# A swin-attention and Fourier-mixing kernel: the attention's transposes for the next row move to the head of the full-array block, and the projection moves ahead of the next image's transposes

## The chip, the cores and the metric

The kernel runs on one core of one Trainium2 chip. The metric is the device time of one execution in microseconds (us), as the median of several runs. The five engines of the core are called by the profile's names: PE is the matrix engine (TensorE) and PEld its weight loads, DVE is VectorE, ACT is ScalarE, POOL is GpSimd, and SP is the engine whose queue issues most DMA transfers.

## The reference

The input is 32 images of 56 x 56 tokens with 128 channels, in float32. Two residual layers follow each other:

```
x = x + attention(group_norm(x))     # layer 0
x = x + fourier(group_norm(x))       # layer 1

attention: roll by (-3,-3); cut into 8 x 8 windows of 7 x 7 = 49 tokens
    qkv = win @ w_qkv.T                       # 4 heads of 32 channels
    a = softmax(q k^T * 32**-0.5 + bias + mask)
    out = (a @ v) @ w_proj.T + b_proj; windows back, roll by (3,3)

fourier: DCT along W, 32 modes, each mode mixed by w0, inverse DCT
    + the same along H with w1
    then relu(h @ W1 + b1) @ W2 + b2          # hidden size 512
```

Everything in an image depends on the norm over that whole image, so the kernel works on three images at a time: one is loaded and transposed, one goes through the attention row by row, one (or two) through the Fourier layer.

## The kernel before

Work goes in cycles. In one cycle, one row of 8 windows of the current image enters the attention (`attn_qk`, `attn_v`, `attn_scores`), the row of two cycles before leaves it (`attn_values`, `attn_project`), and the Fourier layer of the earlier images advances by one step. Eight cycles make one image. Below, "cycle i" is a cycle in which row i (0 to 7) enters.

The order of instructions on PE, ACT, DVE and POOL is the order in which the program writes them. A cycle is written in blocks by the way in which the PE array is divided: `full_first` (whole array), then half columns, quarters and eighths, then `full_last` (whole array again), which runs on into the next cycle's `full_first`. Half columns may come before or after quarters.

```python
def attn_bank():                       # PSUM of the attention: 4 banks in turn
    return bank("pa", 4)

def attn_exp(r):                       # ACT
    nc.scalar.activation(a3, a3, AF.Exp)

def attn_divide(r):                    # DVE sum and reciprocal, then POOL  (L443, L445, L446)
    nc.vector.tensor_reduce(sm, a3, axis=AX.X, op=ALU.add)
    nc.vector.reciprocal(rs, sm)
    nc.gpsimd.tensor_tensor(a3, a3, rs..., ALU.mult)

def attn_transpose(im, i, r):          # softmax rows to columns
    a = a_sb[r % 3]
    im.aT = []
    for hf in range(2):
        pt = attn_bank()
        for h in range(NH):
            nc.tensor.transpose(pt..., a..., ident...)         # L457, 8 in all
        aT = work.tile([P, 4, P], F32, tag="aT", name="aT")
        if hf: nc.scalar.copy(aT..., src)                      # L465, ACT
        else:  nc.vector.tensor_copy(aT..., src)               # L467, DVE
        im.aT.append(aT)

def attn_values(im, i, r):             # 32 small matmuls L482 into two banks, then
    ...                                # oT <- banks: ACT L515, three DVE L513

def attn_project(im, i):               # 3 or 4 matmuls L524 on oT, then
    ...                                # DVE L532 (xl += projection), DMA to scr

def image_groups(im, i):               # next image: 7 transposes L262 into two banks,
    ...                                # ACT copies xw (L280, L274, L275),
                                       # DVE statistics L284, POOL adds b_proj (L289)
```

```python
def full_first(cycle, norm):
    im, i = row(cycle - 2)
    if im:
        attn_transpose(im, i, cycle - 2)
    ...                                        # sums of the row of cycle - 3
    attn_qk(im, i, False)                      # row(cycle): PE L359 (q), L366 (k);
                                               # ACT L362 (q), L371 (k), DVE L379 (k)
    ...
    ff_in(im, FF_AT.index(c))                  # PE L749 (4 matmuls), ACT L757 (hid)
    ...
    attn_divide(cycle - 1)

def quarters(cycle):                           # PE L413, DVE L421; L706
    ...
def half_columns(cycle):                       # PE L391, ACT L398; L633 or L667
    ...
def eighths(cycle):                            # PE L482
    im, i = row(cycle - 2)
    if im:
        attn_values(im, i, cycle - 2)

def full_last(cycle, norm):
    next(norm)
    if row(cycle - 2)[0]:
        last_out(cycle)                        # ff_out: PE L769, DVE L781
    next_image(cycle)                          # image_groups in cycles 3, 4, 5 and 6
    if row(cycle)[0]:
        attn_exp(cycle)                        # ACT L438
    im, j = row(cycle - 2)
    if im:
        attn_project(im, j)
    next(norm)
```

The row maximum and its subtraction (`attn_max`: DVE L431, POOL L432) stand after the eighths in cycles without a feed-forward group and before the half columns in cycles with one. The feed-forward runs in seven of the eight cycles, with groups of 512 tokens and, in cycles 6 and 7, of 320 and 256; cycle 5 has none.

```python
FF_GROUPS = (HB, HB, HB, HB, 320, 256, HB)     # HB = 512
FF_AT = (7, 8, 9, 10, 12, 13, 14)              # step of the Fourier layer; step = cycle number - 10 - 8 * image
```

Of the kernel before, what the change touches and what calls it, by code (L numbers as in the profile page):

```python
# [23 lines left out]
WT = WS * WS  # L24
# [11 lines left out]
JP = 64  # L36
# [12 lines left out]
def swin_fourier_kernel(  # L49
# [33 lines left out]
    def attn_bank():  # L83
        return bank("pa", 4)
# [24 lines left out]
    def load_image(b):  # L109
        t = big.tile([TC, NCH, C], F32, tag="xl", name="xl", bufs=2)  # L110
        h = NCH // 2
        for n0, n1 in ((0, h), (h, NCH)):
            for a, e, p, src in chunks_of(x, b, n0, n1):
                nc.sync.dma_start(t[p, a:e], src)
        return t
# [128 lines left out]
    def image_begin(b):  # L244
        im = Image()
        im.b = b
        im.x = xls.pop(b) if b in xls else load_image(b)
        im.xw = {}
        im.st = small.tile([P, NWR, 6], F32, tag="st0", name="st0", bufs=2)
        im.part = small.tile([TC, 2, C // 4, NWR], F32, tag="part", name="part", bufs=1)  # L250
        im.scr = dram.tile([S, S, C], F32, tag="scr", name="scr", bufs=2)
        return im
# [197 lines left out]
    def attn_transpose(im, i, r):  # L450

        a = a_sb[r % 3]
        im.aT = []
        for hf in range(2):
            pt = attn_bank()
            for h in range(NH):
                nc.tensor.transpose(  # L457
                    pt[:PW, h * P : h * P + PW],
                    a[:PW, h, 2 * hf : 2 * hf + 2].rearrange("p w j -> p (w j)")[:, :PW],
                    ident[:PW, :PW],  # L460
                )
            aT = work.tile([P, 4, P], F32, tag="aT", name="aT")
            src = pt[:PW].rearrange("p (m x) -> p m x", x=P)[:, :, :PW]
            if hf:
                nc.scalar.copy(aT[:PW, :, :PW], src)  # L465
            else:
                nc.vector.tensor_copy(aT[:PW, :, :PW], src)  # L467
            im.aT.append(aT)

    def attn_values(im, i, r):  # L470


        v = v_sb[r % 3]
        po = [attn_bank(), attn_bank()]
        HALF = RT // 2
        po4 = [p[:, :HALF].rearrange("p (r n s) -> p n r s", r=WS, s=WS) for p in po]
        for f in range(2):
            for e in range(2):
                for h in range(NH):
                    for u in range(2):  # L480
                        ks = slice(u * JP, u * JP + WT)
                        nc.tensor.matmul(  # L482
                            po4[u][h * HD : (h + 1) * HD, 2 * f + e],
                            lhsT=v[ks, 2 * f + e, h * HD : (h + 1) * HD],
                            rhs=im.aT[f][ks, h, e * JP : e * JP + WT],
                            start=True,
                            stop=True,
                        )

        if i % 2 == 0:  # L490
            im.oT = work.tile([P, 2 * RT], F32, tag="oT", name="oT")
        oT = im.oT


        oTr = oT[:, i % 2 * RT : (i % 2 + 1) * RT].rearrange("p (r x) -> p r x", x=S)
        for u in range(2):
            src = po[u][:, :HALF].rearrange("p (r f x) -> p r f x", r=WS, f=2)
            x0 = SS + u * 2 * WS
            if not u:
                dst = bass.AP(  # L500
                    oTr.tensor, oTr[:, :, x0:].offset, [oTr.ap[0], [S, WS], [4 * WS, 2], [1, 2 * WS]]
                )
                parts = [(dst, src)]
            else:
                n = S - 4 * WS - x0
                parts = [
                    (oTr[:, :, x0 : x0 + 2 * WS], src[:, :, 0]),
                    (oTr[:, :, S - n : S], src[:, :, 1, :n]),
                    (oTr[:, :, 0:SS], src[:, :, 1, n:]),
                ]  # L510
            for d, f in parts:
                if u:
                    nc.vector.tensor_scalar(d, f, im.bias[:, 2:3], None, ALU.add)  # L513
                else:
                    nc.scalar.activation(d, f, AF.Identity, bias=im.bias[:, 2:3])  # L515

    def attn_project(im, i):

        oT = im.oT
        n0, n1 = WS * i // 2, WS * (i + 1) // 2  # L520
        base = i // 2 * WS
        pp = attn_bank()
        for n in range(n0, n1):
            nc.tensor.matmul(  # L524
                pp[:TC, (n - n0) * C : (n - n0 + 1) * C],
                lhsT=oT[:, (n - base) * TC : (n - base + 1) * TC],
                rhs=wproj,
                start=True,
                stop=True,
            )  # L530
        piece = im.x[:, n0:n1]
        nc.vector.tensor_tensor(  # L532
            piece,
            pp[:TC, : (n1 - n0) * C].rearrange("p (n c) -> p n c", c=C),
            piece,
            ALU.add,
        )
        nc.sync.dma_start(
            im.scr[2 * n0 : 2 * n1].rearrange("(n r) w c -> (r w) n c", r=2), piece
        )  # L540
# [273 lines left out]
    def row(r):  # L814
        return (images[r // NWR], r % NWR) if 0 <= r < NB * NWR else (None, 0)

    def fourier(cycle):

        b, c = divmod(cycle - CONV_BEGIN, NWR)
        return [(images[b - k], c + k * NWR) for k in (1, 0) if 0 <= b - k < NB]  # L820
# [5 lines left out]
        return []  # L826

    def full_first(cycle, norm):
        im, i = row(cycle - 2)
        if im:  # L830
            attn_transpose(im, i, cycle - 2)
        last, j = row(cycle - 3)
        if last:
            sums = attn_sums(last, j)
            next(sums)
        im, i = row(cycle)
        if im:
            attn_qk(im, i, False)
        for im, c in fourier(cycle):
            for width, g in back_groups(c):  # L840
                load_modes(im, width, g)
        next(norm)
        if last:
            next(sums)
        for im, c in fourier(cycle):
            if c == 0:
                im.stats = fourier_stats(im)
                im.cols = {}
                next(im.stats)
                load_columns(im, 0)  # L850
                load_columns(im, 1)
        for im, c in fourier(cycle):
            if c in FF_AT:
                ff_in(im, FF_AT.index(c))
        for im, c in fourier(cycle):
            if c == 0:
                next(im.stats)
        if row(cycle - 1)[0]:
            attn_divide(cycle - 1)
# [29 lines left out]
    def eighths(cycle):  # L889
        im, i = row(cycle - 2)  # L890
        if im:
            attn_values(im, i, cycle - 2)

    def last_out(cycle):
        for im, c in fourier(cycle):
            if c in FF_AT:
                ff_out(im, FF_AT.index(c))

    def full_last(cycle, norm):
        next(norm)  # L900
        if row(cycle - 2)[0]:
            last_out(cycle)
        next_image(cycle)
        if row(cycle)[0]:
            attn_exp(cycle)
        im, j = row(cycle - 2)
        if im:
            attn_project(im, j)
        next(norm)

    def next_image(cycle):
        b, i = divmod(cycle, NWR)
        if b + 1 < NB:
            if i == 2:
                images[b + 1] = image_begin(b + 1)
            for j in {3: (0,), 4: (2,), 5: (4,), 6: (6,)}.get(i, ()):
                image_groups(images[b + 1], j)
# [3 lines left out]
    def first_rows(cycle, norm):  # L921
        im, i = row(cycle)
        if im:
            attn_qk(im, i, True)
        if cycle:
            attn_exp(cycle - 1)
        next(norm)
        last, j = row(cycle - 3)
        if last:
            attn_project(last, j)  # L930
        im2, i2 = row(cycle - 2)
        if im2:
            attn_transpose(im2, i2, cycle - 2)
        if cycle:
            attn_divide(cycle - 1)
        if im:
            attn_scores(im, i, cycle)
            attn_max(cycle)
        if im2:
            attn_values(im2, i2, cycle - 2)  # L940
        if last:
            for _ in attn_sums(last, j):
                pass
        if im:
            attn_v(im, i, cycle)
        next(norm)
        next_image(cycle)
        if cycle == CONV_BEGIN - 1:
            attn_exp(cycle)
            attn_project(im2, i2)  # L950
        next(norm)

    def nothing():
# [4 lines left out]
    with tc.manual_schedule(engines={ET.PE, ET.Activation, ET.DVE, ET.Pool}):  # L958
# [6 lines left out]
        for cycle in range(NB * NWR + CONV_BEGIN + FF_AT[-1] - NWR + 1):  # L965
# [21 lines left out]
            b, i = divmod(cycle, NWR)  # L987
# [66 lines left out]
```

## Time and profile before

| What | Value |
|---|---|
| median of 3 runs | 3668.28 us (3667.28 to 3670.64) |
| span of the profiled run | 3669.3 us |
| instructions | 139900 |
| DVE busy | 2222.3 us (61%) |
| ACT busy | 2152.8 us (59%) |
| POOL busy | 1371.9 us (37%) |
| mean granted PE clock | 0.996 |
| HBM traffic over the span | 103 GB/s |

Busy times are sums over the whole span. Where one engine waits for another, the row of waits names the waiting instruction, the one that released it, and the total, the number and the longest of these waits. A timeline row has the start, the duration, the engine, the source line, what is written from what, the shapes, how often it is repeated without a break, and in brackets the idle time before it with the instruction that ended it. A matmul on float32 data can appear as two records. Durations of successive PE rows overlap, because a matmul's end is modelled and the next one starts before it; so the time that a group takes on PE is read here as the difference between the starts of two rows that follow each other.

### The profile page before, as it was taken

The page shows a single profiled execution, that of the slowest core. Times are in us where ns is not written, and L with a number is a line of the kernel's source. Part 1 is how long each engine was busy: PE and PEld are TensorE (multiplying, and loading weights), DVE is VectorE, ACT ScalarE, POOL GpSimd, SP SyncE. Part 2 cuts the span into 40 slices and gives each one's busy share as a digit, 9 for nine tenths or more (in the row PEclk, how much of TensorE's full clock was granted, in tenths as well). Part 3 has the DMA queues.
Part 4 walks back from the last instruction along what each step waited for, and adds up shares of the span by engine and source line. Part 5 has one row for each costly group of instructions (what it writes and reads, how often), then busy time and mean ns, then how long its engine had stood idle before and what let it go on. Part 6 is the DMA issues. An engine that isn't in the chain of part 4 may idle for free.

```text
span 3669.3 us, 139900 instructions
## 1 busy us (share of the span) xinstructions
PE 3603.8 (98%) x61184; PEld 2938.0 (80%) x61184; DVE 2222.3 (61%) x4741; ACT 2152.8 (59%) x4043; POOL 1371.9 (37%) x1421
## 2 busy tenths in 40 slices
PE   7899999999999999999999999999999999999998
PEld 5687888888888888888888888878888888888786
DVE  7766666656666566666566665666656666656641
ACT  5565556655565656566555666565665565665653
POOL 5433334333334333343333343333343333433321
PEclk9999999999999999999999999999999999999999
DMA  4334443433433334334434334443344343443333
GB/s 116 97 102 111 107 109 93 118 106 102 115 97 106 108 106 113 105 98 118 106 101 117 97 108 107 109 111 99 103 110 110 102 115 98 111 108 106 96 108 90
DMA packets 687795, 388.93 MB, mean 106 GB/s; under 512 B 40495, under 2 KB 658128, under 8 KB 686928
## 3 DMA queue, kind: packets, MB, share of 16 engines
q1 hardware_dynamic: 686573, 379.65, 38.1%
q8 instruction: 482, 7.90, 0.9%
q14 instruction: 129, 1.06, 0.1%
q10 hardware_dynamic: 611, 0.32, 0.0%
HBM read 218.29 MB, written 161.48 MB: 103 GB/s over the span
## 4 chain that ended last, share of the span: by engine, by line
PE 91%; DVE 4%; ACT 2%; POOL 1%; issue 1%; DMA 0%; SPq 0%; POOLq 0%; DVEq 0%; ACTq 0%
PE pc L769 21%; PE pc L749 17%; PE pa L391 7%; PE pc L667 6%; PE pc L633 6%; PE pa L413 6%; PE pa L457 5%; PE pc L706 5%; PE pa L524 5%; PE pa L482 4%; PE pa L359 4%; PE pa L366 4%; PE pa L262 2%; POOL a L432 1%; DVE a L421 1%; DVE mx L431 1%
## 5 line engine op out<-in xcount | busy, mean ns | idle before, releaser
L769 PE MATMUL pc<-wff,hid 128*128 128x128 f32 (+1 forms) x6400 | 779.1, 279 | 1.0 <-ACT hid L757 0.9
L446 POOL TENSOR_TENSOR a<-a,rs 128x784 f32<-128x784 f32 x256 | 389.6, 1522 | 993.0 <-DVE rs L445 869.7
L769 PEld LDWEIGHTS pc<-wff,hid 128*128 128x128 f32 (+1 forms) x6400 | 731.1, 189 | 24.0 <-issue 2.9
L749 PE MATMUL pc<-xf,wff 128*128 128x512 f32 (+2 forms) x1792 | 710.9, 539 | 0.9 <-DVE xf L717 0.6
L757 ACT ACTIVATE hid<-pc,b1sb 128x512 f32<-128x512 f32 (+2 forms) x896 | 536.4, 635 | 93.0 <-PE pc L749 89.4
L749 PEld LDWEIGHTS pc<-xf,wff 128*128 128x128 f32 x1792 | 339.5, 190 | 310.3 <-issue 229.4
L432 POOL TENSOR_TENSOR a<-a,mx 128x784 f32<-128x784 f32 x256 | 388.8, 1519 | 456.9 <-DVE mx L431 448.0
L781 DVE TENSOR_TENSOR res<-pc,res 128x512 f32<-128x512 f32 (+3 forms) x259 | 144.1, 568 | 607.7 <-issue 293.9
L289 POOL TENSOR_TENSOR xl<-xl,bproj 112x512 f32<-112x512 f32 (+1 forms) x256 | 286.0, 1138 | 347.3 <-PE pa L262 338.8
L421 DVE TENSOR_TENSOR a<-pa,bm 128x392 f32<-128x392 f32 x512 | 259.7, 550 | 203.2 <-PE pa L413 203.1
L438 ACT ACTIVATE a<-a 128x784 f32<-128x784 f32 x256 | 225.0, 879 | 222.3 <-POOL a L432 221.9
L379 DVE TENSOR_SCALAR k<-pa,heads,bqkv 128x392 f32<-128x392 f32 x246 | 168.6, 685 | 288.0 <-ACT k L371 288.0
L465 ACT COPY aT<-pa 113x452 f32<-113x452 f32 x256 | 137.5, 537 | 303.0 <-PE pa L457 298.7
L398 ACT COPY v<-pa 128x512 f32<-128x512 f32 x256 | 152.5, 596 | 268.4 <-PE pa L391 268.3
L739 POOL TENSOR_TENSOR res<-res,b2sb 128x512 f32<-128x512 f32 (+2 forms) x256 | 263.7, 1035 | 98.5 <-DMA res<-scr 88.3
L413 PEld LDWEIGHTS pa<-k,q 64*64 64x64 f32 x8192 | 183.6, 132 | 137.7 <-DVE rs L445 67.5
L513 DVE TENSOR_SCALAR oT<-pa,bqkv 128x98 f32<-128x98 f32 (+2 forms) x768 | 170.6, 278 | 200.0 <-PE pa L482 200.0
L391 PE MATMUL pa<-wn,xw 128*64 128x128 f32 x4096 | 282.5, 280 | 5.4 <-DVE a L421 2.9
L391 PEld LDWEIGHTS pa<-wn,xw 128*64 128x64 f32 x4096 | 220.3, 137 | 55.5 <-issue 16.4
L524 PE MATMUL pa<-wproj,oT 128*112 128x128 f32 x1792 | 241.0, 274 | 12.6 <-DVE oT L513 7.2
L431 DVE TENSOR_REDUCE mx<-a 128x16 f32<-128x784 f32 x256 | 247.3, 966 | 5.5
L443 DVE TENSOR_REDUCE sm<-a 128x16 f32<-128x784 f32 x256 | 245.7, 960 | 5.0 <-ACT a L438 5.0
(91 smaller groups left out, 5899.7 us busy)
## 6 DMA issues: line engine op xcount, KB each, us to landing
zscr<-z SPq DMA_DIRECT2D x512, 112.0 KB
htok<-scr SPq DMA_DIRECT2D x256, 196.0 KB
zT<-zscr SPq DMA_DIRECT2D x192, 256.0 KB
res<-scr SPq DMA_DIRECT2D x160, 256.0 KB
out_dram<-res SPq DMA_DIRECT2D x128, 256.0 KB
scr<-xl SPq DMA_DIRECT2D x128, 224.0 KB
xl<-in_x_dram SPq DMA_DIRECT2D x32, 784.0 KB
xl<-in_x_dram SPq DMA_DIRECT2D x32, 672.0 KB
```

What stands on the lines that cost most here:

```text
L289: nc.gpsimd.tensor_tensor(piece, piece, bproj.unsqueeze(1).to_broadcast([TC, e - a, C]), ALU.add)
L391: nc.tensor.matmul(pv[hs, j * C : (j + 1) * C], lhsT=im.xw[i][:, w * WT : w * WT + JP], rhs=im.w[:, 2 * C : 3 * C], start=True, stop=True,)
L413: nc.tensor.matmul(ps[hp][HALVES[e], pr * 2 * WT : (pr + 1) * 2 * WT], lhsT=q[cs, w * WT : w * WT + JP], rhs=k_sb[cs, :, w], start=True, s ...
L421: nc.vector.tensor_tensor(a[:, 2 * hp : 2 * hp + 2, :, 0:WT].rearrange("p u w j -> p w u j"), ps[hp][:, :RT].rearrange("p (w u j) -> p w u ...
L431: nc.vector.tensor_reduce(mx, a3, axis=AX.X, op=ALU.max)
L432: nc.gpsimd.tensor_tensor(a3, a3, mx.unsqueeze(2).to_broadcast([P, 2 * NWR, WT]), ALU.subtract)
L446: nc.gpsimd.tensor_tensor(a3, a3, rs.unsqueeze(2).to_broadcast([P, 2 * NWR, WT]), ALU.mult)
L524: nc.tensor.matmul(pp[:TC, (n - n0) * C : (n - n0 + 1) * C], lhsT=oT[:, (n - base) * TC : (n - base + 1) * TC], rhs=wproj, start=True, sto ...
L739: nc.gpsimd.tensor_tensor(res[:m, c0:c1], res[:m, c0:c1], b2sb[:m].unsqueeze(1).to_broadcast([m, c1 - c0, C]), ALU.add,)
L749: nc.tensor.matmul(ph[:, :n], lhsT=wff1[:, f * P : (f + 1) * P], rhs=xff[:, t0 : t0 + n], start=True, stop=True,)
L757: nc.scalar.activation(hf[:, :n], ph[:, :n], AF.Relu, bias=b1sb[:, f : f + 1])
L769: nc.tensor.matmul(pf[:m, c * C : (c + 1) * C], lhsT=im.hid[f][:, c * P : c * P + m], rhs=wff2[:, f], start=(f == 0), stop=(f == NF - 1),)
```

## The change

The transposes of a row's softmax (`attn_transpose`) move from the head of the next-but-one cycle to the end of the cycle before it: they are now the first thing in `full_last`, directly after the eighths, and work on the row that has been divided in this cycle. As two rows' transposed tiles may be alive at once in the program text, `im.aT` is kept by row. In `full_last` the projection moves ahead of the next image's transposes and of the exponential. The order of the full-array block on PE becomes: transposes L457, feed-forward output L769, projection L524, next image's transposes L262, then q and k; before, it was L769, L262, L524, L457, then q and k. The counts and shapes of the instructions are the same. The change is meant to give PE work at the head of the block that depends on nothing just computed, and to take the copy of the transposed softmax (ACT L465) out from behind the exponential.

```diff
-        im.xw = {}
+        im.xw, im.aT = {}, {}
...
     def attn_transpose(im, i, r):
         a = a_sb[r % 3]
-        im.aT = []
+        im.aT[i] = []
...
-            im.aT.append(aT)
+            im.aT[i].append(aT)
...
-                            rhs=im.aT[f][ks, h, e * JP : e * JP + WT],
+                            rhs=im.aT[i][f][ks, h, e * JP : e * JP + WT],
...
     def full_first(cycle, norm):
-        im, i = row(cycle - 2)
-        if im:
-            attn_transpose(im, i, cycle - 2)
         last, j = row(cycle - 3)
...
+    def transpose_next(cycle):
+        im, i = row(cycle - 1)
+        if im:
+            attn_transpose(im, i, cycle - 1)
...
     def full_last(cycle, norm):
+        transpose_next(cycle)
         next(norm)
-        if row(cycle - 2)[0]:
+        im, j = row(cycle - 2)
+        if im:
             last_out(cycle)
+            attn_project(im, j)
         next_image(cycle)
         if row(cycle)[0]:
             attn_exp(cycle)
-        im, j = row(cycle - 2)
-        if im:
-            attn_project(im, j)
         next(norm)
...
         if cycle == CONV_BEGIN - 1:
             attn_exp(cycle)
             attn_project(im2, i2)
+            transpose_next(cycle)
```

## The prediction

> **What bounds the kernel now.** I read first the busy times and the chain that ended last, on the page:
>
> ```profile
> PE 3603.8 (98%) x61184; PEld 2938.0 (80%) x61184; DVE 2222.3 (61%) x4741; ACT 2152.8 (59%) x4043; POOL 1371.9 (37%) x1421
> ...
> PE 91%; DVE 4%; ACT 2%; POOL 1%; issue 1%; DMA 0%; SPq 0%; POOLq 0%; DVEq 0%; ACTq 0%
> ```
>
> PE is busy for 98% of the span and 91% of the chain lies on it. But a matmul row also covers a wait inside it, so I go on to PE's timeline and take differences between the starts of successive rows. Over the whole span the cycles repeat: an image takes 111.9 to 113.2 us, and the eight cycles take about 14.2, 13.95, 16.0, 15.1, 14.9, 10.4, 14.9 and 12.4 us (i = 0 to 7). The same group takes the same time in almost every cycle (L262 0.72 us, L457 0.79, L359 0.67, L366 0.66, L524 0.65 or 0.87 for 3 or 4 matmuls, L749 3.53 at 512 tokens and 1.82 at 256), so PE streams without a pause nearly everywhere. No instruction is added or removed, and every block keeps its array shape; so only waits can change. I find one place where PE waits in each image, from the end of cycle 5 into cycle 6, here in its PE timeline (start, duration, group):
>
> ```profile
> 1819.80 0.99 PE L262 MATMUL pa<-ident_x,xl 112*128 112x112 f32 x7
> 1820.93 1.10 PE L524 MATMUL pa<-wproj,oT 128*112 128x128 f32 x8
> ...
> 1824.01 2.32 PE L749 MATMUL pc<-xf,wff 128*128 128x320 f32 x8
> 1826.48 0.90 PE L413 MATMUL pa<-k,q 64*64 64x98 f32 x32 [0.15 <-DVE k L379]
> ```
>
> L262 lasts 1.13 us from start to start instead of 0.72: L524 waits 0.41 us for oT. Then L749 with 320 tokens takes 2.47 us, where a line through 1.82 (256) and 3.53 (512) gives 1.82 + 64 x 1.71/256 = 2.25: L413 waits 0.22 us for the DVE copy of k. What makes k late is ACT's queue in the same stretch, and the POOL subtraction ahead of it:
>
> ```profile
> 1823.36 0.88 ACT L438 ACTIVATE a<-a 128x784 f32<-128x784 f32 x1 [1.96 <-POOL a L432]
> 1824.13 0.52 ACT L465 COPY aT<-pa 113x452 f32<-113x452 f32 x1
> 1824.54 0.59 ACT L362 ACTIVATE q<-pa,bqkv 128x392 f32<-128x392 f32 x1
> ```
>
> The exponential could not start before 1823.36, when POOL had finished the subtraction (first row below), and aT, q and k queue up behind it in ACT, until L413 at 1826.48. The second POOL row is the division in cycle 7, which I need below:
>
> ```profile
> 1821.80 1.52 POOL L432 TENSOR_TENSOR a<-a,mx 128x784 f32<-128x784 f32 x1 [3.30 <-DVE mx L431]
> ...
> 1844.72 1.53 POOL L446 TENSOR_TENSOR a<-a,rs 128x784 f32<-128x784 f32 x1 [0.44 <-DVE rs L445]
> ```
>
> **What the Trainium skill says.** "PSUM — Partial Sum Buffer", section "Engine vs sequencer instructions": the queues of ScalarE, VectorE and GpSimd are strictly first in, first out, and matmuls start and finish in program order. The trace agrees: q (L362) waited behind aT although PE had finished L359 at about 1823.5. So the position of an instruction in its queue decides, on both sides. "TensorEngine Tiling (Array Packing)", section "Key Properties": a change of tiling mode drains TensorE. The trace agrees in size: L366 takes 0.75 us before a half-column group and 0.66 before a full-array one, about 0.1 us. The change makes no more such switches. "Trainium Kernel Development and Optimization", section "Performance Expectations": matmul busy time is a bad metric for the distance to the roofline. Here 98% busy does hide the waits above; I don't use it as a bound.
>
> **The change part by part.** Call E the end of the eighths (start of the next PE group), here 1819.80 in cycle 5.
>
> *End of cycle 5, gain.* oT is ready at 1820.12 + 0.66 = E + 0.98 (DVE L513, three instructions), and L524 starts at E + 1.13 whatever PE does before. Before, L262 (0.72) covers part of this; after, L457 (0.79) does: L524 still at E + 1.13. Up to q the rest is the same sum (0.94 + 0.72 against 0.94 + 0.79), so about 0.07 us is won. In cycle 6 the aT copy no longer stands between the exponential and q: the step from L465 to L362 is 1824.54 - 1824.13 = 0.41 us. L413 would be possible at E + 6.27 instead of E + 6.68. PE itself gets there at E + 1.13 + 0.94 + 0.72 + 0.67 + 0.68 + 2.25, about E + 6.4. So 0.26 us are won in cycles 5 and 6. But the next image's transposes come later, and ACT is then free of the xw copies only at E + 3.54 (L262 at E + 2.07, and 1.47 as counted below), while POOL lets the exponential start at E + 3.56: just a tie.
>
> *Cycle 7, loss.* The transposes L262 at the end of cycle 6 now stand directly before q, without L524 and L457 (0.66 + 0.79 us) in between. ACT must copy xw, and only then run the exponential, q and k. In the PE timeline from the end of cycle 6 to that of cycle 7:
>
> ```profile
> 1835.37 0.92 PE L262 MATMUL pa<-ident_x,xl 112*128 112x112 f32 x7
> ...
> 1838.91 1.89 PE L749 MATMUL pc<-xf,wff 128*128 128x256 f32 x8
> 1840.73 0.90 PE L413 MATMUL pa<-k,q 64*64 64x98 f32 x32
> ...
> 1846.22 2.05 PE L769 MATMUL pc<-wff,hid 128*128 128x128 f32 x16
> ```
>
> and in ACT's:
>
> ```profile
> 1836.03 0.49 ACT L280 COPY xw<-pa 128x392 f32<-128x392 f32 x1 [3.12 <-PE pa L262]
> ...
> 1836.84 0.89 ACT L438 ACTIVATE a<-a 128x784 f32<-128x784 f32 x1
> ```
>
> Counted from the start of L262: the first xw copy starts at +0.66 and the exponential at +1.47. The exponential gives way after 0.77 us (cycle 6 above), q takes 0.48, k to the DVE copy 0.72 (DVE's k starts at 1825.74 in cycle 6), that to L413 0.74. The sum is 1.47 + 0.77 + 0.48 + 0.72 + 0.74 = 4.18 us. PE gets to L413 after 0.74 + 0.67 + 0.66 + 1.82 = 3.89 us, because the group in cycle 7 is the shortest. L413 waits 0.29 us. In the cycles that follow the transposes of cycles 3 and 4 it doesn't: L749 takes 3.53 us in cycle 4, and in cycle 5 L391 and L667 stand before L413 (4.5 us).
>
> A second wait in the same cycle: L457 is now the first group after the eighths and needs POOL's division of the row. In seven of the eight cycles that division ends 1.2 to 2.9 us before E, but in cycle 7, where the statistics of the next image's norm sit in front of DVE's sum, it ends at 1844.72 + 1.53 = 1846.25, and E is 1846.22: 0.03 us after. It hangs on DVE's k, which comes before L413 by 0.74 us instead of 0.85, so the division moves to about E + 0.14. From a releaser to the PE group took 0.15 us at L513 to L524. So PE waits about 0.29 us here.
>
> *Start and end, gain.* In cycles 10 to 17, counted from the start of the program, there is no feed-forward yet. In the old order L391 waits for the aT copy in cycles 12 to 15 (0.53 to 0.66 us idle in front of it, 0.7 to 0.85 by starts): about 3.0 us, which disappear. L457 in front of a waiting L524 covers 0.79 us at the ends of cycles 10, 15 and 16, of which the k chain takes back part in the next cycle: 0.45 and 0.4 us remain, and some 1.3 around cycle 17. With 0.4 us at the last row that makes about 5.7 us, once.
>
> *Sum.* The pattern holds for the 29 images in which cycles 5 to 7 have both a feed-forward and a next image. Gain 29 x 0.26 = 7.5 us and 5.7 us; loss 29 x (0.29 + 0.29) = 16.8 us. Net +3.6 us: 3668.3 + 3.6, about 3672 us.
>
> **The rivals.** First, that the waits in cycle 7 don't come: the chains there rest on five steps of 0.5 to 0.8 us each, and if they are 0.3 us shorter in all, what remains is the gain of 13.2 us, 3655 us. For it speaks that the old L413 in cycle 7 never waited; against it, that DVE's k ended only 0.16 us before it. Second, that the loss grows: the attention has four PSUM banks in turn, and the bank that a tile gets depends on which is freed first. In cycle 6 the copy of k takes a bank that ACT, not DVE, had read last; if it is the one of the second half of the transposes, L366 waits for L275, which would end about 0.4 us later than L366 could begin. That is 29 x 0.4 = 12 us more, 3684 us. Third, that it makes no difference at all, because PE's stream is the bound and both waits are hidden by the drain at the array switches: then only the 5.7 us of the start are left, 3663 us. A transfer could also come late, as SP's queue is reordered and the projection's store is issued 0.79 us nearer to the next cycle; but the load for the feed-forward is issued 10 us before POOL uses it (1.27 us), so I give that little weight.
>
> **Range and chances.** The two losses and the gain are each uncertain by about half: a loss of 0.3 to 0.9 us per image in cycle 7 and a gain of 0.1 to 0.3 give -6 to +23 us over 29 images; less 5.7 us for the start that is -12 to +17. I widen below only a little, for the first rival, and take 3655 to 3687. Two per cent are 73 us, or 2.4 us per image: nothing found is of that size. So within 2% 0.98, and 0.01 for each side.
>
> **What would show it.** In the changed profile: (1) L413 of cycle 7 has a wait for DVE's k (row L413 <- DVE k L379 grows from 3.5 us, or L749 with 256 tokens takes 2.1 us by starts instead of 1.82); (2) L457 of cycle 7 waits for POOL L446 (0.3 us in total before, some 8 after); (3) L749 with 320 tokens falls from 2.47 to about 2.25 us; (4) L457 then L524 at the end of cycle 5 start 1.13 us apart; (5) L391's waits for aT (2.4 us) are gone. Wrong would be: an image of under 111.7 or over 112.8 us, or a group other than these that grows.

## The result and the profile after

The changed kernel takes 3680.11 us (median of 6 runs, 3677.76 to 3683.42) against 3668.3 us before (6 runs): a ratio of 1.0031, with a 95% interval of 1.0018 to 1.0044. It is slower by 0.3%. The predicted time was 3672 us with a range of 3655 to 3687. Repeated later beside the other experiments, the changed kernel measured 1.0041 (1.0029 to 1.0053).

The busy times and the chain of the changed kernel, from its page:

```profile
PE 3606.5 (98%) x61184; PEld 2941.2 (80%) x61184; DVE 2226.2 (60%) x4741; ACT 2128.6 (58%) x4043; POOL 1372.0 (37%) x1421
...
PE 87%; DVE 6%; DMA 2%; POOL 2%; ACT 2%; issue 1%; SPq 0%; ACTq 0%; POOLq 0%; DVEq 0%
```

PE's busy time has hardly changed, but the chain now has 2% of DMA, where it had 0%, and DVE has gone from 4% to 6%. Where the time went is seen from starts to starts. The table gives what changes in PE's stream: the mean time in one cycle for 28 images in the middle of each trace, and the sum over them. A cycle is counted from one start of L359 (q) to the next. The whole span of the two traces differs by 10.7 us.

| PE group, by starts | before | after | over 28 images |
|---|---|---|---|
| cycle 5, all | 10.40 | 10.33 | -2.0 us |
| cycle 6, L749 (320 tokens, until L413) | 2.45 | 2.25 | -5.7 us |
| cycle 6, L706 | 1.67 | 2.01 | +9.7 us |
| cycle 7, L749 (256 tokens, until L413) | 1.83 | 2.09 | +7.3 us |
| cycle 7, L482 (until the next group) | 0.74 | 0.92 | +5.1 us |
| cycle 7, all | 12.45 | 12.79 | +9.5 us |
| all eight cycles (24 to 247) | 3142.5 | 3158.2 | +15.7 us |
| from the start to cycle 24 | 278.5 | 275.7 | -2.8 us |
| from cycle 248 to the end | 243.1 | 240.9 | -2.2 us |

(Cycle 7 gains back 0.1 us behind the two waits: L769 there takes 1.80 us in place of 1.89. Scattered waits add 1.6 us in the rest of cycle 6 and some 3 us in cycles 2 to 4.)

First the end of cycle 5 and cycle 6 in PE's timeline of the changed kernel:

```profile
1374.64 1.03 PE L457 MATMUL pa<-ident,a 113*113 113x113 f32 x8
1375.69 1.10 PE L524 MATMUL pa<-wproj,oT 128*112 128x128 f32 x8
...
1378.67 2.32 PE L749 MATMUL pc<-xf,wff 128*128 128x320 f32 x8
1380.92 0.91 PE L413 MATMUL pa<-k,q 64*64 64x98 f32 x32
1381.65 2.06 PE L706 MATMUL pc<-idcth,zT 64*64 64x112 f32 x64
1383.64 1.09 PE L391 MATMUL pa<-wn,xw 128*64 128x128 f32 x16
```

and, from the kernel before, L706 in the image whose lines the prediction shows:

```profile
1827.20 1.73 PE L706 MATMUL pc<-idcth,zT 64*64 64x112 f32 x64
1828.86 1.09 PE L391 MATMUL pa<-wn,xw 128*64 128x128 f32 x16
```

L457 and the wait for oT together fill 1.05 us, then L524 (L457 itself starts 0.82 us after L482, so that L524 comes 1.87 us after the start of L482, as before). L749 now takes 1380.92 - 1378.67 = 2.25 us and L413 follows without a wait for k. But L706 takes 1383.64 - 1381.65 = 1.99 us from start to start, where it took 1828.86 - 1827.20 = 1.66. That wait was not in the prediction. It stands in the middle of L706, where the second of the two loads of zT comes into use, and it varies: over the 28 images L706 takes from 1.64 us (no wait) to 2.59.

Then cycle 7, in PE's and ACT's timelines of the changed kernel:

```profile
1391.69 0.87 PE L262 MATMUL pa<-ident_x,xl 112*128 112x112 f32 x7
...
1393.72 1.89 PE L749 MATMUL pc<-xf,wff 128*128 128x256 f32 x8
1395.81 0.91 PE L413 MATMUL pa<-k,q 64*64 64x98 f32 x32 [0.20 <-DVE k L379]
```

```profile
1392.29 0.49 ACT L280 COPY xw<-pa 128x392 f32<-128x392 f32 x1 [3.46 <-PE pa L262]
...
1393.11 0.89 ACT L438 ACTIVATE a<-a 128x784 f32<-128x784 f32 x1
1393.87 0.60 ACT L362 ACTIVATE q<-pa,bqkv 128x392 f32<-128x392 f32 x1
```

The exponential starts 1.42 us after L262 and q 0.76 us later, all in one queue behind the xw copies; k is late, and L413 comes 4.12 us after L262 and waits (L749 takes 2.09 us). At the end of the same cycle, in PE's and POOL's timelines:

```profile
1400.56 0.81 PE L482 MATMUL pa<-aT,v 49*32 49x49 f32 x64
1401.48 1.05 PE L457 MATMUL pa<-ident,a 113*113 113x113 f32 x8
```

```profile
1399.91 1.52 POOL L446 TENSOR_TENSOR a<-a,rs 128x784 f32<-128x784 f32 x1 [0.44 <-DVE rs L445]
```

The division ends at 1401.43, and L457 starts 0.05 us later; L482 takes 0.92 us instead of 0.74.

### The profile page after: what moved, and what is told of

It reads as the page before. It is cut to its first block, busy times and chain, and to the rows that moved or that the text cites. A ratio compares the mean times of both kernels' runs of the same rounds, so it can differ in the third digit from the quotient of the medians.

```text
span 3680.0 us, 139841 instructions
## 1 busy us (share of the span) xinstructions
PE 3606.5 (98%) x61184; PEld 2941.2 (80%) x61184; DVE 2226.2 (60%) x4741; ACT 2128.6 (58%) x4043; POOL 1372.0 (37%) x1421
## 4 chain that ended last, share of the span: by engine, by line
PE 87%; DVE 6%; DMA 2%; POOL 2%; ACT 2%; issue 1%; SPq 0%; ACTq 0%; POOLq 0%; DVEq 0%
PE pc L769 19%; PE pc L749 17%; PE pa L457 6%; PE pa L391 6%; PE pc L633 6%; PE pa L524 5%; PE pa L413 5%; PE pa L359 4%; PE pc L667 4%; PE pa L366 4%; PE pa L482 4%; PE pc L706 4%; PE pa L262 2%; POOL a L446 1%; DMA zT<-zscr 1%
## 5 line engine op out<-in xcount | busy, mean ns | idle before, releaser
L769 PE MATMUL pc<-wff,hid 128*128 128x128 f32 (+1 forms) x6400 | 760.5, 276 | 1.0 <-ACT hid L757 0.9
L769 PEld LDWEIGHTS pc<-wff,hid 128*128 128x128 f32 (+1 forms) x6400 | 732.3, 190 | 10.0 <-issue 2.9
L446 POOL TENSOR_TENSOR a<-a,rs 128x784 f32<-128x784 f32 x256 | 389.4, 1521 | 911.0 <-DVE rs L445 885.3
L749 PE MATMUL pc<-xf,wff 128*128 128x512 f32 (+2 forms) x1792 | 710.7, 539 | 0.9 <-DVE xf L717 0.6
L749 PEld LDWEIGHTS pc<-xf,wff 128*128 128x128 f32 x1792 | 339.3, 190 | 310.0 <-issue 221.6
L362 ACT ACTIVATE q<-pa,bqkv 128x392 f32<-128x392 f32 x256 | 150.4, 588 | 283.2 <-PE pa L359 281.6
L513 DVE TENSOR_SCALAR oT<-pa,bqkv 128x98 f32<-128x98 f32 (+2 forms) x768 | 170.2, 276 | 218.2 <-PE pa L482 218.2
L413 PEld LDWEIGHTS pa<-k,q 64*64 64x64 f32 x8192 | 183.2, 132 | 139.8 <-DVE rs L445 45.5
L391 PE MATMUL pa<-wn,xw 128*64 128x128 f32 x4096 | 281.9, 280 | 3.4 <-DVE a L421 3.4
L280 ACT COPY xw<-pa 128x392 f32<-128x392 f32 x128 | 62.3, 486 | 380.1 <-PE pa L262 380.1
L457 PE MATMUL pa<-ident,a 113*113 113x113 f32 x2048 | 267.4, 274 | 7.9 <-POOL a L446 3.3
L391 PEld LDWEIGHTS pa<-wn,xw 128*64 128x64 f32 x4096 | 219.8, 137 | 53.2 <-ACT xw L275 16.2
```

Of the source, the lines that this page charges most:

```text
L391: nc.tensor.matmul(pv[hs, j * C : (j + 1) * C], lhsT=im.xw[i][:, w * WT : w * WT + JP], rhs=im.w[:, 2 * C : 3 * C], start=True, stop=True,)
L413: nc.tensor.matmul(ps[hp][HALVES[e], pr * 2 * WT : (pr + 1) * 2 * WT], lhsT=q[cs, w * WT : w * WT + JP], rhs=k_sb[cs, :, w], start=True, s ...
L446: nc.gpsimd.tensor_tensor(a3, a3, rs.unsqueeze(2).to_broadcast([P, 2 * NWR, WT]), ALU.mult)
L457: nc.tensor.transpose(pt[:PW, h * P : h * P + PW], a[:PW, h, 2 * hf : 2 * hf + 2].rearrange("p w j -> p (w j)")[:, :PW], ident[:PW, :PW],)
L749: nc.tensor.matmul(ph[:, :n], lhsT=wff1[:, f * P : (f + 1) * P], rhs=xff[:, t0 : t0 + n], start=True, stop=True,)
L769: nc.tensor.matmul(pf[:m, c * C : (c + 1) * C], lhsT=im.hid[f][:, c * P : c * P + m], rhs=wff2[:, f], start=(f == 0), stop=(f == NF - 1),)
```

## The experiments

They ran in two groups, each beside many runs of the kernel before, which took 3675.3 and 3675.4 us there. The ratios are compared, therefore, and an expectation in microseconds is read as its ratio to 3668.3.

**Transposes moved, projection left in place.**

```diff
     def full_last(cycle, norm):
         transpose_next(cycle)
         next(norm)
         im, j = row(cycle - 2)
         if im:
             last_out(cycle)
-            attn_project(im, j)
         next_image(cycle)
         if row(cycle)[0]:
             attn_exp(cycle)
+        if im:
+            attn_project(im, j)
         next(norm)
```

> The transposes of the next row at the head of the block, but the projection stays behind the next image's transposes (order L457, L769, L262, L524). Theory (the loss comes from the projection's move: its store slips ahead of a load in SP's queue, and the xw copies come too late for cycle 7): no wait of L413 in cycle 7 (L749 with 256 tokens back at 1.82 us), no wait of L706 in cycle 6 (1.65 us), and in cycle 5 L457 and L262 together cover the whole wait for oT, so that cycles 5 and 6 gain 0.41 us an image, bounded by the chain over the exponential. L457 in cycle 7 still waits some 0.1 us for the division. About 3656 us. Rival (the transposes' move itself costs, by its wait for the division or by the banks): 3672 us or more.

Measured 0.9977 (0.9969 to 0.9984), faster than both kernels; expected was 3656, or 0.9966. PE's timeline at the end of cycle 5:

```profile
1366.52 1.03 PE L457 MATMUL pa<-ident,a 113*113 113x113 f32 x8
1367.38 0.87 PE L262 MATMUL pa<-ident_x,xl 112*128 112x112 f32 x7
1368.18 1.13 PE L524 MATMUL pa<-wproj,oT 128*112 128x128 f32 x8
1369.14 0.82 PE L359 MATMUL pa<-xw,wn 128*128 128x392 f32 x2
```

L457, L262 and L524 follow each other with no more than 0.08 us of wait: two groups lie between the eighths and L524, where each of the other orders has at most one. In the means of the trace, L749 of cycle 7 is 1.82 us and L482 there 0.75, L706 of cycle 6 is 1.69, and cycles 5 and 6 take 25.05 us instead of 25.32 before. So the move of the transposes alone is a gain, and the loss comes when the projection moves as well. The gain was 0.27 us an image instead of 0.41: L457 in cycle 5 and L706 in cycle 6 wait now and then, by 0.1 and 0.05 us in the mean. The rival falls.

**Projection moved, transposes left in place.**

```diff
     def full_last(cycle, norm):
         next(norm)
-        if row(cycle - 2)[0]:
-            last_out(cycle)
-        next_image(cycle)
-        if row(cycle)[0]:
-            attn_exp(cycle)
         im, j = row(cycle - 2)
         if im:
+            last_out(cycle)
             attn_project(im, j)
+        next_image(cycle)
+        if row(cycle)[0]:
+            attn_exp(cycle)
         next(norm)
```

> The projection ahead of the next image's transposes, but the transposes of the softmax stay at the head of the next cycle (order L769, L524, L262, L457). Theory: in cycle 5 L524 comes straight after the eighths and waits 1.13 us for oT uncovered, so L413 of cycle 6 is 0.5 us later than before; in cycle 7 L413 just doesn't wait; about 3682 us. Rival (the store ahead of both loads of modes costs what it costs in the changed kernel): L706 in cycle 6 waits too, 3690 us.

Measured 1.0044 (1.0031 to 1.0058), where the theory's 3682 us is 1.0037 and the rival's 1.006. PE's timeline at the end of cycle 5:

```profile
1377.04 0.81 PE L482 MATMUL pa<-aT,v 49*32 49x49 f32 x64
1378.91 1.10 PE L524 MATMUL pa<-wproj,oT 128*112 128x128 f32 x8 [1.06 <-DVE oT L513]
```

L524 starts 1.87 us after L482, in place of the 0.74 us that L482 needs: 1.13 us with nothing to cover them. L706 of cycle 6 takes 1.65 us: the theory holds and the rival falls. In cycle 7 L749 takes 1.82 us and L482 0.74. So this loss is not that of the changed kernel: none of the three waits L706, L749 and L482 comes with the projection's move alone, nor (but for a few late loads) with the transposes' alone. They need both. For the next question this run decides nothing: the store stands ahead of both loads here, but PE also comes to L706 later, 8.68 us after the start of L482 in the mean against 7.89 in the changed kernel, and the second load is issued 3.83 us before L706 instead of 2.92.

**The loads of modes ahead of the store.** The orders of PE, ACT, DVE and POOL stay those of the changed kernel; only SP's is put back.

```diff
     def full_first(cycle, norm):
...
         for im, c in fourier(cycle):
-            for width, g in back_groups(c):
-                load_modes(im, width, g)
+            if c != 4:
+                for width, g in back_groups(c):
+                    load_modes(im, width, g)
...
     def full_last(cycle, norm):
         transpose_next(cycle)
         next(norm)
+        for im, c in fourier(cycle):
+            if c == 3:
+                for width, g in back_groups(4):
+                    load_modes(im, width, g)
```

> The changed kernel, with the two loads of modes for cycle 6 written at the end of cycle 5, so that SP issues both ahead of the projection's store, as the kernel before does; PE, ACT, DVE and POOL keep their order. Theory (the queue's order makes the second load late): L706 in cycle 6 back at 1.65 us from 1.99, the waits in cycle 7 stay; about 3671 us. Rival (PE only arrives earlier than the data in any order): L706 keeps its wait, 3680 us.

Measured 1.0009 (1.0001 to 1.0017); 3671 us is 1.0007. The SP timelines of one image show the cause (L688 loads the modes, L538 is the projection's store). Before:

```profile
1374.58 0.94 SPq L688 DMA_DIRECT2D zT<-zscr  x2
1375.62 0.44 SPq L538 DMA_DIRECT2D scr<-xl  x1
```

After the change:

```profile
1377.65 0.39 SPq L688 DMA_DIRECT2D zT<-zscr  x1
1378.13 0.45 SPq L538 DMA_DIRECT2D scr<-xl  x1
1378.63 5.51 SPq L688 DMA_DIRECT2D zT<-zscr  x3
```

In this experiment, and PE there:

```profile
1377.33 0.94 SPq L688 DMA_DIRECT2D zT<-zscr  x2
1378.37 0.44 SPq L538 DMA_DIRECT2D scr<-xl  x1
```

```profile
1380.13 0.90 PE L413 MATMUL pa<-k,q 64*64 64x98 f32 x32
1380.85 1.71 PE L706 MATMUL pc<-idcth,zT 64*64 64x112 f32 x64
1382.49 1.09 PE L391 MATMUL pa<-wn,xw 128*64 128x128 f32 x16
```

Before, both loads are issued and then the store. After, the store stands between the first and the second load, in all 28 images (the x3 in that row are the second load and the two of cycle 7). With the order put back, L706 takes 1382.49 - 1380.85 = 1.64 us again (mean over the images 1.71, from 2.01; 4 of the 28 images still wait), though PE reaches it as early as in the changed kernel, 7.85 us after the start of L482 in the mean, against 7.89. So it is the queue's order, not PE's earlier arrival. In the mean the second load is issued 1.16 us after the first in the changed kernel and 0.43 us after it here. Whether it is late through this later issue or because it follows the store's 224 KB was not separated.

**All three repairs.** To the loads come the exponential ahead of the next image's copies (except in cycle 5, where it waits for POOL), and, in cycle 7 alone, the transposes behind the feed-forward output.

```diff
     def full_last(cycle, norm):
-        transpose_next(cycle)
+        late_t = cycle % NWR == 7
+        if not late_t:
+            transpose_next(cycle)
         next(norm)
+        ...                                  # loads of modes, as above
         if im:
             last_out(cycle)
+        if late_t:
+            transpose_next(cycle)
+        if im:
             attn_project(im, j)
+        late = cycle % NWR == 5
+        if row(cycle)[0] and not late:
+            attn_exp(cycle)
         next_image(cycle)
-        if row(cycle)[0]:
+        if row(cycle)[0] and late:
             attn_exp(cycle)
```

> The changed kernel with three repairs: loads of modes ahead of the store; the exponential ahead of the next image's copies in ACT's queue in every cycle but 5; in cycle 7 the transposes of the softmax behind the feed-forward output. Theory (the loss is the sum of the three waits): L706 1.65 us in cycle 6, L749 1.82 and L482 0.74 us in cycle 7, the gain of cycles 5 and 6 stays; about 3658 us. Rival (the waits only hide others of the same size): 3668 us or more.

Measured 0.9967 (0.9955 to 0.9980); 3658 us is 0.9972. PE's timeline from cycle 6 to cycle 7:

```profile
1374.89 1.71 PE L706 MATMUL pc<-idcth,zT 64*64 64x112 f32 x64
1376.53 1.09 PE L391 MATMUL pa<-wn,xw 128*64 128x128 f32 x16
...
1386.62 1.89 PE L749 MATMUL pc<-xf,wff 128*128 128x256 f32 x8
1388.44 0.90 PE L413 MATMUL pa<-k,q 64*64 64x98 f32 x32
```

L706 takes 1.64 us and L749 1.82 us, and L482 of cycle 7 is at 0.74 us in the mean; cycle 7 takes 12.34 us. The three waits are the loss: with them gone, the reordering is faster than the kernel before.

**The changed kernel once more.** No edit; it stands beside the next three.

> The changed kernel unchanged, beside the next three on one chip, so that their differences are read from one set of runs. Every theory expects the ratio on record again, 1.003 of the kernel before, with L706 of cycle 6 near 2.0 us and L749 of cycle 7 at 2.09 us.

Measured 1.0041 (1.0029 to 1.0053), within the interval of the first time; L706 of cycle 6 was 2.02 us, L749 of cycle 7 2.09.

**The exponential alone.** Of the three repairs, only that of the exponential.

```diff
+        late = cycle % NWR == 5
+        if row(cycle)[0] and not late:
+            attn_exp(cycle)
         next_image(cycle)
-        if row(cycle)[0]:
+        if row(cycle)[0] and late:
             attn_exp(cycle)
```

> The changed kernel, with the exponential ahead of the next image's copies in ACT's queue in every cycle but 5. Theory (xw copies, exponential, q and k in a row make k late in cycle 7): L749 of cycle 7 back at 1.82 us from 2.09; DVE's chain then starts 0.1 us earlier before L413, so L482 there falls from 0.92 to about 0.82; L706 in cycle 6 stays near 2.0. Some 0.37 us in each of 29 images: a ratio of 1.000. Rival (k waits for PE or for its bank, not for ACT's queue): L749 stays at 2.09, ratio 1.003.

Measured 1.0020 (1.0012 to 1.0028), where 1.000 was expected. In PE's timeline of cycle 7 L413 no longer waits:

```profile
1393.71 1.89 PE L749 MATMUL pc<-xf,wff 128*128 128x256 f32 x8
1395.53 0.91 PE L413 MATMUL pa<-k,q 64*64 64x98 f32 x32
```

L749 takes 1.82 us and L482 of that cycle fell to 0.82 us, as the theory said, so that cycle 7 is 0.37 us shorter. But L706 of cycle 6 waits still more, 2.11 us in place of 2.02, and takes back 2.4 us over 28 images. The mechanism is right, the gain was set too high; the second load is issued 2.79 us before L706 in the mean, where it was 2.94, and why is open.

**Cycle 7's transposes alone.** Of the three repairs, only that in cycle 7.

```diff
-        transpose_next(cycle)
+        late_t = cycle % NWR == 7
+        if not late_t:
+            transpose_next(cycle)
         ...
         if im:
             last_out(cycle)
+        if late_t:
+            transpose_next(cycle)
+        if im:
             attn_project(im, j)
```

> The changed kernel, with the transposes of the softmax behind the feed-forward output in cycle 7 alone. Theory (the division ends too late for them): L482 of cycle 7 falls from 0.92 to 0.74 us, L749 of cycle 7 stays at 2.09, L706 in cycle 6 near 2.0; 0.18 us in each of 29 images, a ratio of 1.0015. Rival (the longer L482 is the price of the array switch into a transpose): the 0.18 us appear at L482 in cycles 0 to 6 too, which they do not in the trace, and don't go away here.

Measured 1.0027 (1.0017 to 1.0036), where 1.0015 was expected. That is 0.0014 under the changed kernel in the same group, but the two intervals overlap; the trace decides. At the end of cycle 7 in PE's timeline:

```profile
1403.82 0.81 PE L482 MATMUL pa<-aT,v 49*32 49x49 f32 x64
1404.56 2.05 PE L769 MATMUL pc<-wff,hid 128*128 128x128 f32 x16
```

L482 takes 0.74 us, L749 of the cycle stays at 2.08: the wait for the division has gone and the other stays. The longer L482 was not the price of the switch.

**Transposes moved, with the repairs that fit.** The first experiment, with the loads ahead of the store and cycle 7's transposes behind the output, each edited as above.

> The version with the transposes moved and the projection left in its place, with two additions: in cycle 7 the transposes behind the feed-forward output, and the loads of modes written ahead of the store. Theory: the waits of cycle 7 are gone in the version without additions already (12.35 us), so the additions bring at most the few late loads (0.05 us an image); ratio 0.997, the same as without them. Rival (the late loads there were chance, and a further wait is hidden behind them): 0.995 or 0.999.

Measured 0.9967 (0.9955 to 0.9979). L706 is at 1.68 us and cycle 7 at 12.33, as without the additions (1.69 and 12.34); the intervals 0.9955 to 0.9979 and 0.9969 to 0.9984 overlap, so that the additions bring nothing that is shown.

## Why the prediction was right or wrong

- *"Gain 29 x 0.26 = 7.5 us" in cycles 5 and 6.* Right in place and size: 7.7 us over 28 images. The step from L413 at E + 6.68 to about E + 6.4 is what the trace shows (L749 2.25 us).
- *L413 in cycle 7, 0.29 us.* Right: 0.26 us, and 4.12 us from L262 where 4.18 was counted. The exponential's experiment shows that ACT's order makes it.
- *L457 in cycle 7, 0.29 us.* Right in mechanism, too big: 0.18 us. The division did move, by what was counted. The term mis-sized is the 0.15 us from a releaser to the PE group, taken from L513 to L524; from POOL to L457 it was 0.05. And the two waits in cycle 7 gave back 0.1 us behind them, so that the cycle lost 0.34 us instead of 0.58.
- *Start and end, 5.7 us.* Too big: 2.8 us until cycle 24, and 2.2 us from cycle 248 to the end. The waits of L391 for aT did disappear, but new ones appeared before L457, L482 and L524 in the cycles without feed-forward. The 2.2 us at the end also hold the 130 us after the last attention row, which the prediction did not count. There one L706 waits for its DMA by 2.64 us before and by 0.97 after; in all the runs with both moves this wait is 1.0 to 1.1 us, in the kernel before and the three runs with one of the moves alone 2.2 to 3.0, so that it may well belong to the change. Why is open.
- *"I give that little weight", of a transfer that comes late.* Here the prediction failed. It looked at one of the transfers on SP's queue, the load for the feed-forward, and didn't go through the others, though it named the queue's reordering and the projection's store itself. In its place the runs showed 9.7 us lost to the second load of modes, the largest single loss; putting SP's order back takes nearly all of it away. The prediction's own sign of being wrong, a group other than those named that grows, came true with L706.
- The other signs: (1), (3) and (5) are in the trace. (2) is there by starts alone, 5.1 us instead of 8; the rows of waits name POOL L446 for only 3.3 us of L457, all of it in cycles 12 to 16. (4) is 1.05 us instead of 1.13, because L457 itself starts 0.08 us later.
- The rivals: the first (no wait in cycle 7) and the third (nothing changes but the start) fall. The second, a bank that delays k in cycle 6, did not happen: L366 there takes 0.66 us in the mean and L749 2.25 us in every image. A loss near to the 12 us that this rival named did come, but from another cause.
- One sum of the range is wrong: a loss of 0.3 and a gain of 0.3 us per image give 0 and not -6 us, so that the lower end came out 6 us too low. And L413 in cycle 7 did wait once before the change: L749 took 1.99 us in one of the 28 images.

The measured time was 8 us above the predicted one. A loss left out (9.7 us) and a start gain set too high (2.9 us), less a loss in cycle 7 set too high (7.3 us), are 5 us of it; scattered waits of under 0.1 us a cycle add 4, the end takes 2 off, and 1 us is the difference between the two profiled runs and the medians. That the time lies well inside the range is in part luck, as two errors of 7 to 10 us had opposite signs.

## What to carry to other kernels

On a saturated engine, ask of each moved block what else had been using the time in front of it: here two groups between the next image's transposes and q had been hiding a chain through ACT, in the one cycle with the shortest block after it. Go through every queue in the new order, the DMA queue too, and for each load whose place changes count the time until its use. And take a compound reordering apart: one half of this one was a gain of 0.2% alone (0.3% with two additions that brought nothing that is shown), the other a loss of 0.4% alone, and the three waits of the whole stand in neither half, so that they had to be looked for in the whole.

## What was not expected

PE's waits named "issue", in which it waits for nothing that the profile shows, stand mostly at two groups of many small matmuls in cycle 2 (a few of L482 in cycle 3). The rows of waits on PE before:

```profile
PE pc L633 <- issue: 3.8, 6, 1.0
...
PE pa L482 <- issue: 3.0, 4, 1.5
```

and after:

```profile
PE pa L482 <- issue: 8.4, 14, 1.3
...
PE pc L633 <- issue: 1.3, 1, 1.3
```

The sum of the two rows is 6.8 us before, 6.5 with the projection moved alone, and 9.7 to 14.4 us in each of the seven kernels with the transposes first (9.7 and 13.9 in the two runs of the changed kernel). It is small, and it moves from L633 to L482. What PE waits for can be read from the DMA packets. Both pages have this row among the queues (packets, MB, share of time):

```profile
q8 instruction: 482, 7.90, 0.9%
```

Its packets are blocks of 16 KB. In the ten traces each of the 172 waits at these two groups ends 1.2 to 1.8 us after such a block has been moved, where 8 to 9% of moments picked at random do. So PE seems to wait there for its own instructions. No run tests it, and why it happens more often with the transposes first is open.
